# Layer 2's pair weights stand three groups ahead of the pair's products

## The chip, the cores and the metric

The kernel runs on one core of a Trainium2 chip. The metric is the device time of one execution in microseconds (us). Engines are named as in the profile: PE is TensorE (PEld its weight loads), ACT is ScalarE, DVE is VectorE, POOL is GpSimd, SP is SyncE.

## What is computed

A graph network of two attention layers and a two-layer perceptron, on 6250 nodes and 100,000 edges that come sorted by their destination, with a self-loop at each node. All numbers are float32. Cut to what matters:

```python
def gat_conv(x, src, dst, W, a_src, a_dst, bias, heads):
    h = (x @ W).reshape(n, heads, -1)
    alpha_s = (h * a_src[None]).sum(-1)
    alpha_d = (h * a_dst[None]).sum(-1)
    e = leaky_relu(alpha_s[src] + alpha_d[dst], 0.2)
    e = exp(e - segment_max(e, dst)[dst])
    alpha = e / (segment_sum(e, dst)[dst] + 1e-16)
    return segment_sum(h[src] * alpha, dst) + bias

h = maximum(layernorm(x), 0)
h = relu(gat_conv(h, src, dst, W1, ..., heads=4))    # 768 -> 256, layer 1
h = relu(gat_conv(h, src, dst, W2, ..., heads=1))    # 256 -> 256, layer 2
h = relu(h @ Wm1 + bm1)                              # 256 -> 256
out = x + h @ Wm2 + bm2                              # 256 -> 768
```

## The kernel before

**Tiles.** The nodes are cut into 49 node tiles of 128. The edges are cut into 782 edge tiles of 128; four edge tiles make a group (TPG = 4, NG = 196 groups), two of them a pair, so a group has pairs 0 and 1. Four groups, 16 edge tiles, carry on average the edges of one node tile. A layer's loop runs over the groups; each turn has two half-groups, one for each pair.

**One pair in layer 2.** POOL gathers the source nodes' rows from a table in HBM, one indirect DMA of 128 rows for each edge tile (`gather`, L666). A row holds the 256 features, the score, a one and the score's multiple. ACT makes the edge weights w: for each of the two tiles one Relu (L733) and one Exp (L735). DVE puts each edge's weight in the column of its destination (L739, `hw`). PE multiplies `hw` with the gathered rows G and adds into `o_ps` in PSUM (L760); each of the two float32 products shows as two passes in the profile.

**Sums and node steps.** Two groups share one `o_ps`. `take_sum` adds it into a running sum (DVE L777) and copies quarters of it to the node tiles that they belong to (ACT L786). When a node tile's sum is whole, `Node2.steps` carries it through the rest in six steps:

- step 0: self-loop and reciprocal on DVE (L1082, L1094)
- step 1: `o` on ACT (L1097), then two transposes on PE (L942)
- step 2: `rT` on ACT (L948), then the products with Wm1 on PE (L1106)
- step 3: `mT` on ACT (L1111); then on PE the bias into `y_ps` (L1055) and the first half of the product with Wm2 (L1116)
- step 4: DVE adds x to that half (L1120, called add_x below); then PE does the second half (L1055, L1116)
- step 5: DVE adds x to the second half (L1120), and SP sends the tile out

**The order.** Each engine runs its instructions in the order in which the program writes them, so the program's text is the schedule. The loop writes for each group: the gather of the group 8 ahead (AHEAD), pair 0, the node steps that are due, a sum if one is due; then pair 1, the steps and the sum of that half-group. Which half-group a sum or a step is due at is written out: sum u at half-group 4u + 11 (UP_AT), the six steps of node tile t at 8t + 19 plus 1, 2, 5, 8, 11 and 14 (STEPS_AT), with another table for the last node tiles. So every eight half-groups, over one node tile, the same things recur. Counted from 8t + 19 as position 3, so that a position is the half-group's number modulo 8, they are:

| position | what is written after the pair of this half-group |
|---|---|
| 0 | step 2 (rT, L1106) |
| 1 | step 5 (second add_x, out) |
| 2 | nothing |
| 3 | step 3 (mT, L1055, L1116), a sum |
| 4 | step 0 |
| 5 | step 1 (o, transposes) |
| 6 | step 4 (first add_x, L1055, L1116) |
| 7 | a sum |

The last two groups are written by `last_pairs`.

**Buffers.** 20 pairs of gathered rows fit in SBUF, so a gather waits until the pair 20 pairs before it has been multiplied; since gathers run 8 groups ahead of the pair being written, up to 40 edge tiles are gathered or under way. `w` has 4 buffers, `hw` 14 pairs, `o_ps` three banks. The transposes' PSUM tile `tp` and `y_ps` share two banks (tag "n") in turn; so step 3's L1055 of a node tile needs the add_x of step 5 of the node tile before.

In layer 1 `pair` does other work on DVE (L746 to L748) and nothing on ACT.

Of the kernel before, what the change touches and what calls it, by code (L numbers as in the profile page):

```python
# [30 lines left out]
NG = NQ  # L31
# [24 lines left out]
SOON_FROM, SOON_HELD = min(SOON), 16  # L56
BARE = 8
SLOPES, SLOPES_AT = 56, 150


UP_AT = {4 * u + 11: u for u in range(NU - 16)}
# [10 lines left out]
def kernel(  # L72
# [247 lines left out]
    def rows_in(layer):  # L320

        return gp.tile([P, 2, max(TW.values())], F32, name="G")[:, :, :TW[layer]]
# [40 lines left out]
    def soon_back(i):  # L363
        G = rows_in(1)
        nc.sync.dma_start(G.rearrange("p t c -> p (t c)"), soon_d[i])
        return G
# [242 lines left out]
    def fetch_rows(r):  # L609

        if r < NET // 16:
            drow[r] = rowsp.tile([P, 16 * P], BF16, name="drow")
            nc.sync.dma_start(drow[r], bcast(dmod_d, 16 * P, r * 16 * P))
# [19 lines left out]
    def layer_edges(layer, H, node, pre, matched, pre_pool):  # L633
# [4 lines left out]
        with tc.tile_pool(name=f"eg{layer}", bufs=5) as eg, \  # L638
# [12 lines left out]
            def tiles(g):  # L651

                return range(max(TPG * g, FIRST) - TPG * g, min(TPG * g + TPG, LAST) - TPG * g)

            def gather(g):
                if not 0 <= g < NG:
                    return
                for t in tiles(g):
                    k = TPG * g + t
                    soon = layer == 1 and k // 2 in SOON_AT  # L660
                    if k // 2 not in G:
                        G[k // 2] = (soon_back(SOON_AT[k // 2]) if soon else
                                     first_G.get(layer, {}).get(k // 2) or rows_in(layer))
                    if soon or k < FIRST + len(THERE.get(layer, ())):
                        continue
                    nc.gpsimd.indirect_dma_start(  # L666
                        out=G[k // 2][:, k % 2], out_offset=None, in_=table[layer],
                        in_offset=bass.IndirectOffsetOnAxis(ap=src_i[:, k:k + 1], axis=0))
# [51 lines left out]
                    e_ps[t][:, T, 3 * H:4 * H],  # L720
                    e_ps[t][:, T, :3 * H].rearrange("p t (h k) -> p t h k", k=3), AX.X, ALU.add)

            def pair(g, p):

                if 2 * p not in tiles(g):
                    return
                Gp = G.pop(TPG // 2 * g + p)
                if layer == 2:
                    u = g // 2
                    rows = slope[u // 8][:, u % 8 * P:(u % 8 + 1) * P]  # L730
                    w = sm.tile([P, 2, P], F32, name="w")
                    for t in range(2):
                        nc.scalar.activation(w[:, t], rows, AF.Relu, bias=Gp[:, t, HID + 2:])  # L733
                    for t in range(2):
                        nc.scalar.activation(w[:, t], w[:, t], AF.Exp, bias=Gp[:, t, HID:HID + 1])  # L735
                    hw = hwp.tile([P, 2, P], F32, name="hw")
                    for t in range(2):
                        k = TPG * g + 2 * p + t
                        nc.vector.scalar_tensor_tensor(hw[:, t], iota_ps, dcol[:, k:k + 1], w[:, t],  # L739
                                                       ALU.is_equal, ALU.mult)  # L740
                else:
                    e1, e2 = Gp[:, :, RW[1]:RW[1] + 4], Gp[:, :, RW[1] + 4:]
                    at = TPG * (g % 4) + 2 * p
                    rho, v, w = (e_ps[g // 4][:, at:at + 2, k * H:(k + 1) * H] for k in range(3, 6))
                    nc.vector.tensor_mul(v, e2, rho)
                    nc.vector.tensor_max(w, v, e1)  # L746
                    hw = hwp.tile([P, 2, H, C + 1], F32, name="hw")
                    nc.vector.tensor_mul(  # L748
                        hw, Gp[:, :, :RW[1]].rearrange("p t (h c) -> p t h c", h=H),
                        w.unsqueeze(3).to_broadcast([P, 2, H, C + 1]))  # L750
                u = g // 2
                if u not in o_ps:
                    o_ps[u] = ps.tile([P, RW[layer]], F32, name="o_ps", tag="o", bufs=3)
                for t in range(2):
                    k = 2 * p + t
                    if layer == 2:
                        l, r = hw[:, t], Gp[:, t]
                    else:
                        l, r = hot[g][:, k], hw[:, t].rearrange("p h c -> p (h c)")
                    nc.tensor.matmul(o_ps[u], l, r[:, :RW[layer]], start=(g % 2 == 0 and k == 0),  # L760
                                     stop=(g % 2 == 1 and k == tiles(g)[-1]))
# [36 lines left out]
            def gather_up(u):  # L798

                if u == NU - 1:  # L800

                    late.append(node.steps(NT - 1, None, run[0], o_ps.pop(u)))
                    return
                acc = take_sum(u)
                if u == NU - 2:
                    carry_over(acc)
# [45 lines left out]
            def last_pairs():  # L852

                acc = take_sum(NU - 2)
                before, = late
                pair(NG - 2, 0)
                next(before)
                carry_over(acc)
                next(before)
                next(before)  # L860
                pair(NG - 2, 1)
                next(before)
                pair(NG - 1, 0)
                pair(NG - 1, 1)
                last = node.steps(NT - 1, None, run[0], o_ps.pop(NU - 1))
                for of in (last, before, last, before, last, before, before, last, last):
                    next(of, 0)
                late.clear()

            for g in range(NG):  # L870
                t, j = divmod(g, 4)
                if layer == 2 and g >= NG - 2:
                    if g == NG - 2:
                        last_pairs()
                    continue
                if g == NG - 2:
                    at_end.append(g)
                gather(g + AHEAD)
                pair(g, 0)
                if g == NG - 1:  # L880
                    pair(g, 1)
                if g == NG - 2:
                    gather_up(NU - 2)
                advance(g)
                if taken_up(2 * g) is not None:
                    gather_up(taken_up(2 * g))
                if g <= NG - 4:
                    make_hot(g + 1)
                if g in (NG - 4, NG - 3):
                    make_hot(g + 2)  # L890
                if j == 0:
                    if layer == 1:
                        fetch_rows(t + 4)
                    node.prefetch(t)
                    meet(t + 1)
                    if t % 4 == 1:
                        fetch_slopes(t // 4 + 1)
                elif j == (2 if t < NT - 1 else 1):
                    node.ahead(t)
                elif j % 2:  # L900
                    make_mask((g + 7) // 2)
                if layer == 1:
                    for i, at in enumerate(SOON_GROUP):
                        for k, hits_at in ((2 * i, at - 10), (2 * i + 1, at - 6)):
                            if g == hits_at + 3 + (k % 2 == 0):
                                soon_whole(G, k)
                            if g == hits_at:
                                soon_hits(pre_pool, k)
                            if g == hits_at + 1 + (k % 2 == 0):
                                soon_missing(k)  # L910
                        if g == at - 13:
                            soon_sources(pre_pool, i)
                if g == NG - 3:
                    idle_ps.append(ps.tile([P, 4 * P], F32, name="idle_ps", tag="e"))
                if g >= NG - 3:
                    stay_warm(3)
                if g < NG - 1:
                    pair(g, 1)
                advance(g, 1)
                if j == 3:  # L920
                    join(t + 1)
                if taken_up(2 * g + 1) is not None:
                    gather_up(taken_up(2 * g + 1))
                if NG - 3 <= g < NG - 1:
                    stay_warm(3)
                hot.pop(g, None)
                if layer == 1 and g == SLOPES_AT:
                    slopes(pre_pool, 0, SLOPES)
                if layer == 1 and g == NG - 6:
                    first_sources(2)  # L930
# [77 lines left out]
    with tc.tile_pool(name="wmp", bufs=1) as wp, tc.tile_pool(name="x3", bufs=4) as xp, \  # L1008
# [140 lines left out]
        for stage in range(2):  # L1149
            first_hits(pre, 2, stage)  # L1150
        layer_edges(2, 1, Node2(), pre2, matched, pre)

    edges_stack.close()
# [310 lines left out]
```

## Time and profile before

| | us |
|---|---|
| median of 3 runs | 2594.48 |
| lowest and highest of them | 2586.76, 2594.98 |
| profiled execution, its own time | 2557.3 |
| its span in the profile | 2555.5 |

| | PE | DVE | ACT | POOL |
|---|---|---|---|---|
| busy in the whole span, us | 1718.3 | 1239.2 | 865.5 | 1528.5 |
| share of the span | 67% | 48% | 34% | 60% |

The mean granted PE clock was 0.804 of full speed. The profiled execution was 1.4% shorter than the median of the other runs. Layer 1 takes up the time from about 400 us; layer 2's first product starts at 1422.5 us, its last gather at 2503.5 us. In the profile "idle before" is the time for which an engine stood before an instruction, with what released it; "issue" means that nothing in the profile shows the cause, "remote" that it was an event without an instruction beside it. Ends of matmuls are modelled.

### The profile page before, as it was taken

To read this page: it belongs to the slowest core of one execution; us is meant where nothing else is said; L and a number is where in the kernel's file an instruction comes from. 1 tells how busy PE (TensorE), PEld (TensorE's weight loads), DVE (VectorE), ACT (ScalarE), POOL (GpSimd) and SP (SyncE) were. 2 spreads that over 40 slices of the span, in tenths; PEclk is the share of its full clock that TensorE was granted. 3 is DMA by queue.
4 is the path that set the end of the run, shared out by engine and by line. 5 is a ranking of instruction groups with operands and counts; after the bars stand their busy time and mean duration, and the time that the engine had idled before them with its cause. 6 is when DMAs were issued, how large, how long until landed. Compare 5 with 4: busy or idle time off the path is not lost. (4 is left out here: it accounts for less than half of the span.)

```text
span 2555.5 us, 24791 instructions
## 1 busy us (share of the span) xinstructions
PE 1718.3 (67%) x6948; PEld 1232.2 (48%) x6949; DVE 1239.2 (48%) x3356; ACT 865.5 (34%) x2796; POOL 1528.5 (60%) x1666
## 2 busy tenths in 40 slices
PE   9952768668667767758775546566666666656577
PEld 7731646546445545546553334344344444434344
DVE  7742667567666666566674323233233333333233
ACT  6730011011111111111112535455555555556455
POOL 5357465566666666665555566666666666666661
PEclk9975788778778778778877778778878878787778
DMA  9985344344444444444434244444444444444442
GB/s 352 349 269 167 94 130 127 106 130 129 120 127 137 124 121 126 124 122 128 121 84 149 79 119 126 133 135 125 129 137 125 131 135 135 131 127 134 120 132 75
DMA packets 141093, 355.46 MB, mean 139 GB/s; under 512 B 33731, under 2 KB 51324, under 8 KB 140948
## 3 DMA queue, kind: packets, MB, share of 16 engines
q0 software_dynamic: 75072, 211.10, 30.5%
q1 hardware_dynamic: 64506, 141.20, 16.5%
q10 hardware_dynamic: 1370, 1.48, 0.2%
q8 instruction: 59, 0.97, 0.2%
q14 instruction: 86, 0.70, 0.1%
HBM read 314.67 MB, written 38.99 MB: 138 GB/s over the span
## 5 line engine op out<-in xcount | busy, mean ns | idle before, releaser
L666 POOL DMA_INDIRECT G<-table,src_i x1507 | 1436.4, 953 | 851.5 <-issue 382.8
L760 PE MATMUL o_ps<-hw,hot 128*128 128x260 f32 x1564 | 496.5, 452 | 246.0 <-issue 159.7
L760 PE MATMUL o_ps<-G,hw 128*128 128x258 f32 x1564 | 465.8, 439 | 184.0 <-DVE hw L739 109.2
L739 DVE SCALAR_TENSOR_TENSOR hw<-iota_ps,dcol,w 128x128 f32<-128x128 f32 x782 | 247.5, 349 | 549.7 <-ACT w L735 368.7
L760 PEld LDWEIGHTS o_ps<-hw,hot 128*128 128x128 f32 x1564 | 331.9, 221 | 372.7 <-issue 213.1
L786 ACT ACTIVATE sum<-acc 32x260 f32<-32x260 f32 (+1 forms) x384 | 159.9, 417 | 1007.0 <-DVE acc L777 642.5
L760 PEld LDWEIGHTS o_ps<-G,hw 128*128 128x128 f32 x1564 | 326.0, 220 | 309.1 <-DVE hw L739 138.0
L390 PE MATMUL missing<-kept,soon_hit 128*128 128x268 f32 x1028 | 266.1, 413 | 50.9 <-issue 50.6
L748 DVE TENSOR_TENSOR hw<-G,e_ps 128x520 f32<-128x520 f32 x391 | 271.9, 695 | 30.6 <-DVE e_ps L746 15.8
L733 ACT ACTIVATE w<-slope,G 128x128 f32<-128x128 f32 x782 | 267.1, 389 | 46.2 <-issue 32.8
L735 ACT ACTIVATE w<-w,G 128x128 f32<-128x128 f32 x782 | 267.7, 388 | 28.9 <-remote 15.8
L1116 PE MATMUL y_ps<-wm,mT 128*128 128x384 f32 x392 | 187.4, 610 | 109.1 <-ACT mT L1111 95.7
L390 PEld LDWEIGHTS missing<-kept,soon_hit 128*128 128x128 f32 x1028 | 207.4, 204 | 102.2 <-issue 63.4
L1116 PEld LDWEIGHTS y_ps<-wm,mT 128*128 128x128 f32 x392 | 79.7, 225 | 217.4 <-ACT mT L1111 101.1
L448 PE MATMUL h_ps<-w,r 128*128 128x264 f32 (+1 forms) x588 | 139.2, 390 | 19.8 <-ACT r L438 13.5
L1120 DVE TENSOR_TENSOR y<-y_ps,xt 128x384 f32<-128x384 f32 (+1 forms) x98 | 54.1, 552 | 190.6 <-remote 157.6
L693 DVE TENSOR_TENSOR hot<-iota_ps,dcol 128x512 f32<-128x512 f32 x196 | 133.6, 682 | 24.4 <-remote 24.4
L448 PEld LDWEIGHTS h_ps<-w,r 128*128 128x128 f32 x588 | 109.1, 192 | 42.7 <-ACT r L438 15.2
L1111 ACT ACTIVATE mT<-tp,bm1c 128x128 f32<-128x128 f32 x98 | 30.4, 361 | 252.0 <-remote 184.0
L397 DVE SCALAR_TENSOR_TENSOR G<-G,soon_ok,missing 128x268 f32<-128x268 f32 x46 | 22.6, 492 | 187.0 <-remote 103.1
L1106 PE MATMUL tp<-rT,wm 128*128 128x128 f32 x392 | 59.6, 301 | 63.9 <-ACT rT L948 46.9
L746 DVE TENSOR_TENSOR e_ps<-e_ps,G 128x8 f32<-128x8 f32 x391 | 68.1, 174 | 53.4 <-remote 25.4
(420 smaller groups left out, 1286.8 us busy)
## 6 DMA issues: line engine op xcount, KB each, us to landing
xt<-in_x SPq DMA_DIRECT2D x96, 384.0 KB
drow<-dmod_d SPq DMA_DIRECT2D x49, 512.0 KB
G<-table,src_i POOLq DMA_INDIRECT x1507
xTt<-in_xT SPq DMA_DIRECT2D x49, 384.0 KB
out<-y SPq DMA_DIRECT2D x48, 384.0 KB
table<-kept SPq DMA_DIRECT2D x49, 134.0 KB
table<-kept SPq DMA_DIRECT2D x49, 129.5 KB
soon_d<-G SPq DMA_DIRECT2D x23, 268.0 KB
```

Source lines behind the costliest of these rows:

```text
L390: nc.tensor.matmul(soon_p[k], hit[:, T - there], kept[T], start=(T == there), stop=(T == NT - 1))
L448: nc.tensor.matmul(h_ps[:, :n], r[:, k], w1[:, k, :n], start=(k == 0), stop=(k == KI - 1))
L666: nc.gpsimd.indirect_dma_start(out=G[k // 2][:, k % 2], out_offset=None, in_=table[layer], in_offset=bass.IndirectOffsetOnAxis(ap=src_i[:, ...
L693: nc.vector.tensor_tensor(hot[g][:, T[0]:T[0] + n], iota_ps.unsqueeze(1).to_broadcast([P, n, P]), dcol[:, k:k + n].unsqueeze(2).to_broadca ...
L733: nc.scalar.activation(w[:, t], rows, AF.Relu, bias=Gp[:, t, HID + 2:])
L735: nc.scalar.activation(w[:, t], w[:, t], AF.Exp, bias=Gp[:, t, HID:HID + 1])
L739: nc.vector.scalar_tensor_tensor(hw[:, t], iota_ps, dcol[:, k:k + 1], w[:, t], ALU.is_equal, ALU.mult)
L746: nc.vector.tensor_max(w, v, e1)
L748: nc.vector.tensor_mul(hw, Gp[:, :, :RW[1]].rearrange("p t (h c) -> p t h c", h=H), w.unsqueeze(3).to_broadcast([P, 2, H, C + 1]))
L760: nc.tensor.matmul(o_ps[u], l, r[:, :RW[layer]], start=(g % 2 == 0 and k == 0), stop=(g % 2 == 1 and k == tiles(g)[-1]))
L786: nc.scalar.activation(done[t][r], acc[r], AF.Copy)
L1116: nc.tensor.matmul(y_ps, mT[:, j], wm2[:, j, s * half:(s + 1) * half], start=False, stop=(j == KH - 1))
```

## The change

The weights of a pair move from `pair` to a new function `weigh`, which is called for the pair three groups ahead in layer 2 (WEIGH = {1: 0, 2: 3}); `pair` takes what `weigh` has stored. Ahead of layer 2's loop `weigh` is called for groups 0 to 2. In layer 1 `weigh` runs where it ran. The numbers of instructions, the buffers and the tables UP_AT and STEPS_AT are the same.

```diff
+WEIGH = {1: 0, 2: 3}
...
-            def pair(g, p):
-
-                if 2 * p not in tiles(g):
+            weighed = {}
+
+            def weigh(g, p):
+
+                if g >= NG or (g, p) in weighed or 2 * p not in tiles(g):
                     return
                 Gp = G.pop(TPG // 2 * g + p)
                 if layer == 2:
...
+                weighed[g, p] = Gp, hw
+
+            def pair(g, p):
+
+                if 2 * p not in tiles(g):
+                    return
+                weigh(g, p)
+                Gp, hw = weighed[g, p]
                 u = g // 2
...
+            for g in range(WEIGH[layer]):
+                for p in range(2):
+                    weigh(g, p)
+
             for g in range(NG):
...
                 gather(g + AHEAD)
+                weigh(g + WEIGH[layer], 0)
                 pair(g, 0)
...
                 if g < NG - 1:
+                    weigh(g + WEIGH[layer], 1)
                     pair(g, 1)
```

What lies between the first two "..." inside `weigh` are the lines of `pair` that made w and hw, unchanged (L727 to L750 of the kernel before).

## The prediction

> **What bounds the kernel now.** I read the windows first, because the change touches only layer 2, which runs from the first product at 1422.5 us to the end. The columns are stretch, length, busy us (and instructions) of PE, PEld, DVE, ACT and POOL, then the granted clock, the DMA share and GB/s.
>
> ```profile
> 1424.00:2504.00 1080.00, 674.14 (x2390) 454.49 (x2389) 341.83 (x1029) 588.74 (x1898) 705.85 (x742) 0.79 0.44 129
> 2504.00:2555.00 51.00, 39.68 (x153) 24.99 (x151) 18.59 (x52) 26.67 (x85) 0.52 (x1) 0.92 0.15 51
> ```
>
> The first row is the body, the second the tail after the last gather. Nobody is full in the body: POOL is busy 705.85 of 1080 us, PE 674. The next view is POOL's timeline beside the others over one node tile. Columns: start, length, instruction, idle before it and what ended that.
>
> ```profile
> 2131.76 1.05 PE L1106 MATMUL tp<-rT,wm 128*128 128x128 f32 x8
> ...
> 2132.65 1.04 PE L760 MATMUL o_ps<-G,hw 128*128 128x258 f32 x4
> ...
> 2139.15 0.95 POOL L666 DMA_INDIRECT G<-table,src_i  x1 [0.30 <-issue]
> 2140.70 0.56 DVE L1120 TENSOR_TENSOR y<-y_ps,xt 128x384 f32<-128x384 f32 x1 [8.33 <-issue]
> 2141.17 1.12 DVE L739 SCALAR_TENSOR_TENSOR hw<-iota_ps,dcol,w 128x128 f32<-128x128 f32 x4
> ...
> 2141.57 2.95 PE L760 MATMUL o_ps<-G,hw 128*128 128x258 f32 x6 [7.89 <-issue]
> ...
> 2143.07 0.63 ACT L1111 ACTIVATE mT<-tp,bm1c 128x128 f32<-128x128 f32 x2 [8.74 <-PE o_ps L760]
> 2143.60 0.94 POOL L666 DMA_INDIRECT G<-table,src_i  x1 [3.50 <-ACT mT L1111]
> ```
>
> PE ended the product of y at 2130.2 (L1116, 2128.62 + 1.56), yet DVE's add of it (L1120) began only at 2140.70; PE ended L1106 at 2132.8, yet ACT's mT began at 2143.07. So signals from PE were seen 10 us late, while POOL issued 16 gathers from 2120.21 to 2139.15 (1.2535 us apart: 0.95 of work, 0.30 "issue") and then stood 3.5 us until it saw products free its buffers. DVE was held at L1120 with the next weights (L739) behind it, and PE stood 7.9 us for those weights. The cycle before (2120.21) looks the same; it lasted 23.39 us, which is 16 x 1.2535 + 3.3: one node tile. In the body 742 gathers take 1079 us, against 742 x 1.2535 = 930 unbroken: about 150 us of pauses, some 48. In the tail, without gathers, PE is busy 39.7 of 51 us and is not seen late.
>
> The waits from 1500 us on (us in total, times, longest):
>
> ```profile
> DVE hw L739 <- ACT w L735: 354.0, 130, 16.9
> ACT mT L1111 <- remote: 184.0, 22, 15.3
> DVE y L1120 <- remote: 157.6, 21, 11.9
> PE o_ps L760 <- DVE hw L739: 100.3, 28, 11.0
> PE y_ps L1116 <- ACT mT L1111: 95.7, 16, 14.2
> PE tp L1106 <- ACT rT L948: 46.9, 6, 10.5
> PE y_ps L1055 <- DVE y L1120: 32.6, 5, 11.6
> ```
>
> The largest row (354) is idle time of an engine that isn't full. What counts is PE's four: 100 us for hw, which the change addresses, and 95.7 + 46.9 + 32.6 = 175 us for node steps, which it does not. Following every PE gap of the body to its cause, I get 367 us: 111 in 18 stops for hw with DVE held at L1120, 33 in short waits for hw, 109 in 19 stops for mT, 63 in 9 for rT, 51 in 10 at L1055.
>
> **What the Trainium skill says.** "Perfetto Trace Analysis", Tensor Engine Instruction: the end shown for a matmul is estimated, and its semaphore update comes after PSUM's acknowledgment and has to propagate. So no bar shows a late signal; the 10 us above agree, but the page gives no such size. "TensorE: Matmul & The Clock Gate", What's actually happening: after about 3.4 us idle the array runs at half clock until it was busy about as long. The trace agrees: after a stop of 7.9 us six passes take 2.95 us, against 1.04 for four before it. "Perfetto Trace Analysis", Optimization Strategy: the same gap repeating can mean that there is no buffer for the next tile; POOL's 3.5 us are that.
>
> **The change part by part.** Nothing is added or removed: per pair ACT still does four activations of 386 ns (0.29 us apart, so 1.17 us), DVE two L739 of 350 ns, PE the same products. The orders of PE, POOL and SP are the same; DMAs and gathers are issued where they were.
>
> 1. Before the loop six pairs' weights stand ahead. PE's first product still waits for pair 0 alone, which ACT does first, and the rows are there (gathers lead by 40 tiles). The other five, 5 x 1.17 = 5.9 us of ACT, delay no node step, since the first sum is taken at half-group 11. I take 0; bounds -2 and +6.
>
> 2. The weights of pair h + 6 stand where those of pair h stood. Ahead of each node step on ACT and DVE stands as much new work as before, so those steps cost 0 more. Queued behind a held L1120, mT or rT is now a weight needed six pairs later. New on DVE: the weight buffers (14) make h + 6 wait for the products of pair h - 8; the sums already wait for the same products, and PE has six pairs in hand: 12 tiles at 0.435 us from start to start at full clock (0.87 at half), 5.2 to 10.4 us. I take 0.
>
> 3. The 18 stops (111 us). Their signal is of y's second half, added at position 1 of 8 in a node tile's half-groups. PE then stopped ahead of position 2; now it runs pairs 2 and 3 and stops at position 3, where L1055 needs the same add_x (its PSUM buffer) and L1116 needs mT. What is late next is exactly that. So a stop does not vanish: PE gains four tiles, 4 x 0.435 = 1.7 us (3.4 at half clock). This shortens the body only if it saves pauses. A tile in a cycle costs 23.39/16 = 1.46 us and without pauses 1.2535, so each tile gained saves 0.21 us: all 18 x 4 = 72 tiles would give 15 us. Where the stop moves for good to position 3, the cycle is 16 tiles again and the gain is 0. I take half, **-7.5 us**.
>
> 4. The short waits for hw (33 us) lie in the stretch after a pause in which PE's signals are seen promptly (under 1.5 us late for some 5 us). Less waiting there puts more of the chain into the prompt stretch and may spare a later stop. Bounds 0 and -33; I take a third, **-11**.
>
> 5. The tail: of 4.4 us in which PE stands there, 3.8 are for hw (2.42, 0.74 and 0.35 are the largest). All go: **-3.8**.
>
> Sum: -7.5 - 11 - 3.8 = **-22 us**. Against the profiled execution (2557.3 us, span 2555.5) that is 2535. The median shown is 2594.5, 1.5% above it; I put the same saving on the median: **2572 us**.
>
> **The rivals.**
> *The pauses fall much more.* hw is 144 of the 367 us that PE stands. If POOL's pauses fall in that share, 150 x 0.39 = 59 us; if POOL never pauses, 150 us, and the body is 930. For it: neither engine is full, so they hold each other, and a PE that is looser by six pairs loosens both. Against it: the stops for mT, rT and L1055 (223 us) depend on PE's own order, which stays. Time -45 to -150: 2445 to 2550.
>
> *The change does not do what it says: the lock of 16.* Each cycle ends at a stop that comes once per node tile, whichever it is, and POOL gets 16 tiles of credit per pause. Cycles that end for hw and for mT have the same 23.39 us, which speaks for it. Then only the tail remains, -4, with some noise: 2587 to 2602.
>
> *Slower: a second stop per node tile.* With hw out of the way PE enters the node steps with its signals elsewhere in POOL's cycle. If a cycle then ends after six or ten tiles (at rT, position 0, then at L1055, position 6) rather than after 16, POOL pauses twice in that tile. Each extra pause costs 3.3 us, and a stop at half clock with it. From three more pauses than are saved (9.9 us) the kernel is slower; if it befalls one tile in six, 8 x 3.3 = +26; one in three, 16 x 3.3 = +53. For it: waits of 10 to 15 us whose place follows no engine's work but the gathers. Against: about 48 pauses for 49 tiles, so no double ones now. Time 2602 to 2650.
>
> **How the numbers follow.** About 0.3% (7.8 us) is what a measurement of this kernel can tell from no change. Likeliest, the sum: -8 to -45, chance 0.40. Pauses fall much more: 0.22. Lock of 16: 0.15. Second stop: 0.23. So faster 0.62, same 0.15, slower 0.23. The range leaves out savings over 110 us (0.05) and losses over 20 us (0.13): 2485 to 2615. The likeliest case alone would give 2550 to 2587.
>
> **What would show it right or wrong.** Right: waits of L760 for hw fall from 100 us to under 20, those of L1116 for mT and of L1055 for y grow by most of what goes; POOL's 742 gathers still break after about 16, in 44 to 47 pauses of 3.5 us; tail under 48 us. The lock: 48 pauses and the body still 1079 us. Much faster: stretches of 30 gathers and more without a pause, POOL busy over 70% of the body. Slower: pauses after six or ten gathers, over 50 in all. Wrong altogether: PE's signals prompt under unbroken gathers, or L760 still waiting for hw by tens of us.

## Result and profile after

The changed kernel takes 2582.44 us (median of 17 runs, 2568.05 to 2591.84) against 2592.56 us for the kernel before (17 runs): ratio 0.9962, 95% interval 0.9945 to 0.9978. That is 10 us less (6 to 14), clear of noise, where 22 us were forecast.

The same program runs in two ways. On some occasions, those of the prediction and of the result among them, the kernel before takes about 2590 us and PE's signals are seen late; on others it takes about 2100 us and they are not. All runs of one comparison belong to one occasion. I call the two **late** and **prompt**. Most experiments fell on a prompt one.

The waits of PE in the profile after, from 1500 to 2500 us (us in total, times, longest). L1072, L1128, L1133 and L1137 are the lines that were L1055, L1111, L1116 and L1120; L736, L738, L742, L771, L788 and L797 were L733, L735, L739, L760, L777 and L786:

```profile
PE y_ps L1133 <- ACT mT L1128: 145.5, 19, 15.2
PE y_ps L1072 <- DVE y L1137: 124.9, 22, 14.8
```

No row of L771 waiting for hw is left; 97 us of it stood in the same stretch before. In its place the waits for mT grew from 96 to 146 us and those at the bias line (L1072) from 33 to 125. The groups of the whole profile say the same (line, engine, instruction, count, busy us, mean ns, then idle before it); first a line of before, then two of after:

```profile
L760 PE MATMUL o_ps<-G,hw 128*128 128x258 f32 x1564 | 465.8, 439 | 184.0 <-DVE hw L739 109.2
```

```profile
L771 PE MATMUL o_ps<-G,hw 128*128 128x258 f32 x1564 | 421.1, 416 | 39.9 <-DVE acc L786 18.8
L1133 PE MATMUL y_ps<-wm,mT 128*128 128x384 f32 x392 | 201.2, 648 | 190.4 <-ACT mT L1128 146.1
```

Where PE stops has moved; how fast layer 2 advances has not. POOL's gathers between 1500 and 2500 us, before and after (line, instruction, count, busy us, mean ns, idle before it):

```profile
L666 POOL DMA_INDIRECT G<-table,src_i x686 | 652.6, 951 | 348.3 <-issue 176.0 <-ACT mT L1111 83.2 <-ACT w L735 37.3
```

```profile
L667 POOL DMA_INDIRECT G<-table,src_i x683 | 646.8, 947 | 353.1 <-issue 212.1 <-ACT mT L1128 61.0 <-ACT w L736 27.8
```

686 and 683 gathers in the same 1000 us: the body gained nothing.

The traces' lists of instructions say more about POOL's pauses. Call it a pause when a gather starts over 1 us later than the usual 1.2535 us after the one before. Layer 2's last 742 gathers hold 51 pauses before and 55 after. Only 18 and 16 of these come after exactly 16 gathers; 9 and 16 come after ten or fewer. Every pause stands before the first gather of a pair, where POOL needs the buffer of the pair 20 pairs earlier. In 50 of the 51 and in all 55, the product that frees this buffer had ended before POOL's last gather even began; POOL went on 12.9 and 13.9 us after that end (medians). So POOL does not stand for PE to reach a product; by these times it stands until it sees that PE made it long ago.

The stretch after the last gather did gain; before and after, cut in the same way:

```profile
2504.40:2555.50 51.10, 39.28 (x151) 24.64 (x149) 18.18 (x52) 26.27 (x84) 0.12 (x1) 0.91 0.15 49
```

```profile
2521.70:2566.30 44.60, 33.37 (x144) 22.28 (x144) 14.61 (x39) 19.05 (x60) 0.10 (x1) 0.97 0.17 56
```

It is 44.6 us long, against 51.1 us: 6.5 us less. The profiled execution as a whole was longer (2568.05 us against 2557.3), since layer 2's first product, up to which the change alters nothing on PE, came 13 us later; from layer 2's first product to the end of the span it took 1130.9 us against 1133.0. So the whole times come from the medians, and the place of a gain from the profiles.

### The profile page after: what moved, and what is told of

Read it like the earlier page. It is cut to its first block, busy times and chain, and to the rows that moved or that the text cites. A ratio compares the mean times of both kernels' runs of the same rounds, so it can differ in the third digit from the quotient of the medians.

```text
span 2566.3 us, 24142 instructions
## 1 busy us (share of the span) xinstructions
PE 1697.2 (66%) x6947; PEld 1236.7 (48%) x6949; DVE 1241.0 (48%) x3356; ACT 866.3 (34%) x2796; POOL 1522.2 (59%) x1666
## 4 chain that ended last, share of the span: by engine, by line
another core or an unknown queue 22%; PE 22%; DVE 20%; ACT 16%; issue 15%; DMA 3%; POOL 2%; SPq 0%; POOLq 0%; DVEq 0%; ACTq 0%
PE o_ps L771 8%; ACT w L736 6%; ACT w L738 6%; PE h_ps L449 4%; DVE hot L694 3%; PE y_ps L1133 3%; DVE hw L751 3%; PE missing L391 3%; DVE soon_hit L381 2%; POOL G L667 2%; DMA G<-table,src_i 2%; DVE e_ps L749 2%; ACT sum L797 2%; DVE acc L788 2%
## 5 line engine op out<-in xcount | busy, mean ns | idle before, releaser
L771 PE MATMUL o_ps<-hw,hot 128*128 128x260 f32 x1564 | 503.9, 458 | 237.5 <-issue 148.9
L797 ACT ACTIVATE sum<-acc 32x260 f32<-32x260 f32 (+1 forms) x384 | 159.9, 417 | 1079.0 <-DVE acc L788 769.1
L742 DVE SCALAR_TENSOR_TENSOR hw<-iota_ps,dcol,w 128x128 f32<-128x128 f32 x782 | 248.8, 349 | 563.9 <-ACT w L738 366.7
L771 PEld LDWEIGHTS o_ps<-hw,hot 128*128 128x128 f32 x1564 | 333.6, 223 | 373.0 <-issue 198.8
L771 PE MATMUL o_ps<-G,hw 128*128 128x258 f32 x1564 | 421.1, 416 | 39.9 <-DVE acc L786 18.8
L771 PEld LDWEIGHTS o_ps<-G,hw 128*128 128x128 f32 x1564 | 326.4, 214 | 124.2 <-issue 37.5
L1133 PE MATMUL y_ps<-wm,mT 128*128 128x384 f32 x392 | 201.2, 648 | 190.4 <-ACT mT L1128 146.1
L738 ACT ACTIVATE w<-w,G 128x128 f32<-128x128 f32 x782 | 269.0, 388 | 49.4 <-ACT w L738 16.6
L736 ACT ACTIVATE w<-slope,G 128x128 f32<-128x128 f32 x782 | 266.8, 388 | 47.4 <-issue 32.8
L1133 PEld LDWEIGHTS y_ps<-wm,mT 128*128 128x128 f32 x392 | 84.2, 238 | 400.1 <-ACT mT L1128 178.4
L1137 DVE TENSOR_TENSOR y<-y_ps,xt 128x384 f32<-128x384 f32 (+1 forms) x98 | 54.1, 552 | 187.0 <-remote 151.2
L1072 PE MATMUL y_ps<-bm2r,ones_r 3*128 3x384 bf16 x98 | 34.4, 354 | 148.0 <-DVE y L1137 126.4
L1128 ACT ACTIVATE mT<-tp,bm1c 128x128 f32<-128x128 f32 x98 | 30.3, 360 | 239.7 <-remote 209.4
L788 DVE SCALAR_TENSOR_TENSOR acc<-acc,keep,o_ps 128x260 f32<-128x260 f32 (+1 forms) x192 | 91.3, 476 | 2.9 <-PE o_ps L771 1.7
```

The source lines that it names most:

```text
L788: nc.vector.scalar_tensor_tensor(acc, run[0], keep[:, u % 2:u % 2 + 1], o_ps.pop(u), ALU.mult, ALU.add)
L797: nc.scalar.activation(done[t][r], acc[r], AF.Copy)
L1133: nc.tensor.matmul(y_ps, mT[:, j], wm2[:, j, s * half:(s + 1) * half], start=False, stop=(j == KH - 1))
```

## Experiments

### The change itself on a prompt occasion

The two kernels as they are. They ran after the runs of the next section, to which the first expectation refers.

> The change itself. On a chip where the kernel before takes about 2590 us: 0.3 to 0.5% faster, POOL pausing after about 16 gathers. On a chip where the kernel before takes about 2103 us and POOL's gathers run unbroken at 1.2535 us: gathers are the bound, PE runs close behind them, and a weight three groups ahead waits for rows that have not landed, with the node steps queued behind it; so 0.4 to 0.6% slower, all of it after the last gather (28 us from the last gather's start to the end, against 17). Rival: the loss of the runs with tail_only and separate y banks came from something else in them, and the change is within 0.1% of before.

> The kernel before, for a profile on the same chip. Where it takes about 2103 us: gathers unbroken, DVE's add_x and ACT's mT within 2 us of the PE product that they need, 17 us from the last gather's start to the end. Where it takes about 2590 us: about 48 pauses of POOL, PE's signals up to 15 us late, as in the profile shown.

Measured: 2110.27 us against 2099.35, ratio 1.0052 (1.0039 to 1.0064). On a prompt occasion the change is **slower** by 11 us. Before and after have the same 599 gathers in the 750 us from 1300 us on, with no pause:

```profile
L666 POOL DMA_INDIRECT G<-table,src_i x599 | 568.5, 949 | 182.5 <-issue 66.7 <-ACT w L735 41.7 <-PE o_ps L760 30.8
```

```profile
L667 POOL DMA_INDIRECT G<-table,src_i x599 | 568.4, 949 | 182.5 <-issue 67.9 <-ACT w L738 43.9 <-PE o_ps L771 28.6
```

568.5 + 182.5 over 599 is 1.254 us each: POOL is the bound, and only what comes after its last gather can differ. From 2070 us, about the last gather's start in both, PE has 55 passes left before the change (first line) and 100 after it (second):

```profile
2070.00:2105.00 35.00, 15.42 (x55) 9.41 (x53) 6.55 (x17) 7.52 (x23) 2.83 (x3) 0.85 0.16 49
```

```profile
2070.00:2105.00 35.00, 26.15 (x100) 16.65 (x99) 8.23 (x20) 8.65 (x26) 0.95 (x1) 0.89 0.17 53
```

The timeline of the changed kernel shows why (start, length, instruction, idle before it and its releaser):

```profile
2067.23 0.40 ACT L736 ACTIVATE w<-slope,G 128x128 f32<-128x128 f32 x1 [1.09 <-DMA G<-table,src_i]
2067.96 0.65 DVE L742 SCALAR_TENSOR_TENSOR hw<-iota_ps,dcol,w 128x128 f32<-128x128 f32 x2 [2.98 <-ACT w L738]
2068.52 0.55 DVE L1137 TENSOR_TENSOR y<-y_ps,xt 128x384 f32<-128x384 f32 x1
2069.12 0.47 PE L1072 MATMUL y_ps<-bm2r,ones_r 3*128 3x384 bf16 x1 [2.58 <-DVE y L1137]
```

A weight on ACT waits for a row that has just landed; DVE waits 2.98 us for that weight; only then comes add_x, for which PE has been standing 2.58 us. The node steps are queued behind weights of a pair whose rows aren't there yet. Counted at each gather's start from 1300 to 2050 us, POOL was 4 to 10 tiles ahead of PE's finished products before the change (median 5) and 12 to 20 after it (median 16). So the lead of three groups, 12 tiles, holds PE 11 tiles back, and that is paid once, at the end: from the last gather's start to the end of the span it took 22.8 us before and 35.6 after. Both are longer than expected (17 and 28); the difference is about as expected.

### Ahead in the tail alone, and in the body alone

```diff
+            def lead(g):
+                return max(0, min(3, g - 180)) if layer == 2 else 0
...
-                weigh(g + WEIGH[layer], 0)
+                for q in range(g, g + lead(g) + 1):
+                    weigh(q, 0)
```

This is the tail alone, cut to pair 0. For the body alone `lead` returns `(3 if g < 180 else 0)` in layer 2.

> Weights stand ahead (1, 2, then 3 groups) only from group 181 on; up to there the order is that of the kernel before. Lock theory (each cycle of POOL is one node tile whatever stops PE; the gain of the change sits after the last gather): the stops for hw of about 110 us stay in the body, the stretch after the last gather is 44 to 48 us as after the change (51 before), and the time is 4 to 10 us under before, equal to the change within 4 us. Rival (the gain comes from saved pauses in the body): within 4 us of before.

> Weights stand three groups ahead up to group 179 and are made just before their products after that. Lock theory: hw waits gone in the body, 742 gathers still in about 1080 us, the stretch after the last gather 50 to 52 us: within 4 us of before. Rival (saved pauses): 6 to 12 us under before, like the change.

Both fell on a prompt occasion, for which the expectations give no number. Tail alone: 2114.03 us against 2102.93, ratio 1.0052 (1.0038 to 1.0065), just like the whole change. Body alone: 2103.15, ratio 0.9999 (0.9991 to 1.0007). So the loss lies wholly in the weights that lead at the end. What either does on a late occasion was **not measured**. After 2070 us tail alone leaves PE 101 passes, body alone 52:

```profile
2070.00:2109.00 39.00, 26.53 (x101) 16.88 (x100) 10.23 (x26) 11.46 (x35) 2.84 (x3) 0.87 0.17 55
```

```profile
2070.00:2109.00 39.00, 15.08 (x52) 9.35 (x52) 6.07 (x16) 7.47 (x23) 2.11 (x3) 0.83 0.13 37
```

### Twice the lead, on a late occasion

```diff
-WEIGH = {1: 0, 2: 3}
+WEIGH = {1: 0, 2: 6}
```

> WEIGH = 6 groups ahead instead of 3. Where before takes about 2100 us (gathers unbroken): if the loss is the node steps standing behind weights that wait for rows, it grows with the lead, one group being four gathers of 1.25 us; 12 us for 3 groups makes 4 us per group, so the stretch from the last gather's start to the end is about 40 us (28 with 3, 17 with 0) and the time 20 to 24 us over before. Rival (a fixed cost of standing ahead): 10 us over before, as with 3. Where before takes about 2590 us, lock theory: no difference in the body to 3 groups; 0 to 15 us under before.

Measured: 2582.46 us against 2584.51, ratio 0.9977 (0.9949 to 1.0004). Its gathers from 1500 to 2500 us, then PE's first wait:

```profile
L667 POOL DMA_INDIRECT G<-table,src_i x682 | 645.8, 947 | 354.6 <-issue 167.0 <-ACT mT L1128 128.3 <-ACT w L736 21.3
```

```profile
PE y_ps L1072 <- DVE y L1137: 313.1, 40, 8.9
```

682 gathers. The stops have moved again: PE stands 313 us at L1072 in 40 stops, for an add_x that is queued behind DVE's weight L742. L742 itself waits 440 us in 48 waits for an event that the profile does not name. From the order of the buffers I take it to be PE's late signal that one of the 14 hw buffers is free. A third place to stop, the same pace. From the last gather's start to the end 45.7 us pass here, 45.4 after the change and 51.9 before it, so the gain at the end is there too, though in the medians the 2 us are not clear of noise.

### Other banks for y, and the node steps spread

`y_ps` takes the two PSUM banks with tag "e", which layer 2 leaves idle, so that L1072 no longer waits for the add_x of the tile before:

```diff
-                if g == NG - 3:
+                if layer == 1 and g == NG - 3:
                     idle_ps.append(ps.tile([P, 4 * P], F32, name="idle_ps", tag="e"))
...
-                y_ps = ps.tile([P, half], F32, name="y_ps", tag="n")
+                y_ps = ps.tile([P, half], F32, name="y_ps", tag="e")
...
-                start_y(1, y_ps)
+                y_ps = start_y(1)
```

> The change, with both halves of y in PSUM banks of their own (the two that layer 2 leaves idle), so that L1055 (L1072 in the kernel after) no longer waits for add_x of the tile before. Lock theory: the stops at that line (137 us in 27 stops) go, those for mT at the same position take them over, cycles stay 16 gathers + 3.3 us: within 6 us of the change. Rival (that line is what bounds the cycle): 20 to 60 us faster than the change.

On a prompt occasion: 2113.04 us against 2102.93, ratio 1.0048 (1.0034 to 1.0062), as the change; it tells nothing of the cycle. Then, with those banks, the steps further apart:

```diff
-STEPS_AT = {t: [8 * t + 19 + k for k in (1, 2, 5, 8, 11, 14)] for t in range(NT - 2)}
+STEPS_AT = {t: [8 * t + 19 + k for k in (1, 2, 8, 15, 17, 19)] for t in range(NT - 2)}
```

> As the run with separate banks, and the node steps spread: STEPS_AT offsets 1, 2, 8, 15, 17, 19 instead of 1, 2, 5, 8, 11, 14, so that PE's transposes and L1106 have 6 and 7 half-groups instead of 3 before PE needs what ACT makes of them. Lock theory: no stop within one node tile is left, so POOL's pauses are no longer tied to 16 tiles; PE's stops fall from about 390 us to under 200, the body from 1080 to 950-1030 us, the whole 50 to 130 us under the change. Rival (the pauses are POOL's or the DMA's own, or late signals hit whatever waits for PE, so that the next wait takes over): within 15 us of the change.

It was run twice more:

> The kernel of the run with separate y banks and the node steps spread to offsets 1, 2, 8, 15, 17, 19, again. Where before takes about 2590 us, by the lock theory: POOL's pauses no longer tied to 16 tiles, PE's stops under 200 us, the whole 50 to 130 us under the change; rival: late signals hit the next wait, within 15 us of the change. Where before takes about 2103 us: 0.6% slower, as measured there.

> Separate y banks and the node steps spread to offsets 1, 2, 8, 15, 17, 19, with the weights three groups ahead. Where before takes about 2590 us, lock theory: within one node tile no place is left at which PE stops for ACT or DVE, so POOL's pauses are no longer tied to 16 gathers; the body per gather falls from 1.46 us to 1.28-1.40, the whole 50 to 130 us under before. Rival (late signals hit the next wait that exists, such as the weight buffers or the sums): 1.44 to 1.47 us per gather, within 15 us of before. Where before takes about 2100 us: 0.6 to 0.8% slower, as measured there.

All three comparisons fell on prompt occasions: 1.0061, 1.0076 and 1.0062 times before, 0.1 to 0.25% above the change alone. Offsets 1, 2, 9, 17, 18, 20 leave more room:

> Separate y banks and the node steps spread further: STEPS_AT offsets 1, 2, 9, 17, 18, 20, so 7 half-groups between the transposes and L1106 and 8 between L1106 and mT's product, more than the 16 tiles of a cycle together with the node products. Where before takes about 2590 us, lock theory: PE's stops under 150 us, gathers at 1.26 to 1.38 us each with pauses rarer than one per node tile, the whole 60 to 150 us under before. Rival (late signals hit the next wait): 1.44 to 1.47 us per gather, within 15 us of before. Where before takes about 2100 us, gathers being the bound: 0.6 to 1% slower, by the later node steps at the end.

> Separate y banks and STEPS_AT offsets 1, 2, 9, 17, 18, 20, for a chip where before takes about 2590 us. Lock theory: PE's stops under 150 us, gathers at 1.26 to 1.38 us each with pauses rarer than one per node tile, the whole 60 to 150 us under before. Rival (late signals hit the next wait): 1.44 to 1.47 us per gather, within 15 us of before. Where before takes about 2100 us: 0.5% slower, as measured there.

Prompt both times (1.0048 and 1.0044), and then a late one:

> As the run before of this kernel. Where before takes about 2590 us, lock theory: PE's stops under 150 us, gathers at 1.26 to 1.38 us each with pauses rarer than one per node tile, the whole 60 to 150 us under before. Rival (late signals hit the next wait): 1.44 to 1.47 us per gather, within 15 us of before. Where before takes about 2100 us: 0.5% slower, as measured there.

Measured there: 2570.70 us against 2575.54, ratio 0.9979 (0.9957 to 1.0001). The gain of 60 to 150 us did not come; the time is within 15 us of before, as the rival says. Gathers from 1500 to 2500 us, and PE's first wait:

```profile
L667 POOL DMA_INDIRECT G<-table,src_i x684 | 647.8, 947 | 353.0 <-issue 279.5 <-ACT w L738 40.9 <-PE o_ps L771 9.4
```

```profile
PE o_ps L771 <- DVE acc L788: 291.9, 41, 8.2
```

684 gathers. The waits at L1072 are down to 5 us and those at L1133 to 47 (5 put down to mT, 42 to a weight on ACT), and PE now stands 292 us in 41 stops for an o_ps bank. One cycle shows how:

```profile
2019.24 0.95 POOL L667 DMA_INDIRECT G<-table,src_i  x1 [0.30 <-issue]
2023.21 0.56 DVE L1137 TENSOR_TENSOR y<-y_ps,xt 128x384 f32<-128x384 f32 x1 [7.54 <-remote]
2023.68 0.47 DVE L788 SCALAR_TENSOR_TENSOR acc<-acc,keep,o_ps 128x258 f32<-128x258 f32 x1
2023.85 0.94 POOL L667 DMA_INDIRECT G<-table,src_i  x1 [3.66 <-issue]
2024.21 5.50 PE L771 MATMUL o_ps<-G,hw 128*128 128x258 f32 x16 [7.58 <-DVE acc L788]
```

DVE was held 7.5 us at add_x, now one or two half-groups after its product, with the sum that frees the bank queued behind it; everything was released about 4 us after the start of POOL's last gather. POOL started at 2000.49 and 2023.85 again: 23.36 us, 16 gathers and a pause. Of this kernel's 48 pauses 40 come after exactly 16 gathers, and of the 50 with the lead of six groups 34. In both, too, every pause stands before the first gather of a pair, and in all but one of the 98 the product that frees the buffer had ended before POOL's last gather began.

### No wait within a node tile

The step that was still close was moved too: offsets 1, 2, 9, 17, 18, 24 up to node tile 34, both halves of y made together in two banks, both add_x together in the last step.

The step that makes y, as it is there (cut):

```diff
+                if t < NT - 11:
+                    ys = [start_y(s) for s in range(2)]
+                    for s in range(2):
+                        for j in range(KH):
+                            product(ys[s], s, j)
+                    yield 1
+                    yield 1
+                    for s in range(2):
+                        add_x(ys[s], s)
...
```

> As the far spread, and add_x too stands 7 half-groups after its product: offsets 1, 2, 9, 17, 18, 24 up to node tile 34, both halves of y made together in two banks and both add_x together in the last step; x rows fetched one node tile later. No wait of PE, ACT or DVE on PE's work is left closer than 6 half-groups. Where before takes about 2590 us, lock theory: PE runs on, catches up with the gathers, POOL's pauses vanish for long stretches, 1.255 to 1.35 us per gather, the whole 60 to 150 us under before. Rival (the pauses are POOL's or the chip's own): 16 gathers and a pause of 3.5 us as ever, 1.44 to 1.47 us per gather, within 15 us of before. Where before takes about 2100 us: 0 to 1% slower.

> As the run before of this kernel (offsets 1, 2, 9, 17, 18, 24, halves of y together in two banks). Where before takes about 2590 us, lock theory: POOL's pauses vanish for long stretches, 1.255 to 1.35 us per gather, the whole 60 to 150 us under before. Rival (the pauses are POOL's or the chip's own): 16 gathers and a pause of 3.5 us as ever, 1.44 to 1.47 us per gather, within 15 us of before. Where before takes about 2100 us: 0.5% slower, as measured there.

> As the two runs before of this kernel. Where before takes about 2590 us, lock theory: POOL's pauses vanish for long stretches, 1.255 to 1.35 us per gather, the whole 60 to 150 us under before. Rival (the pauses are POOL's or the chip's own): 16 gathers and a pause of 3.5 us as ever, 1.44 to 1.47 us per gather, within 15 us of before. Where before takes about 2100 us: 0.4 to 0.5% slower, as measured there.

Three comparisons, all on prompt occasions: 1.0054, 1.0036 and 1.0044 times before. What it does on a late one was **not measured**. With the weights just in time from group 180 on:

> The kernel with no wait within a node tile (offsets 1, 2, 9, 17, 18, 24, halves of y together), and weights three groups ahead only up to group 179, just in time after that. Where before takes about 2590 us, lock theory: 1.255 to 1.35 us per gather, 60 to 150 us under before; rival: 1.44 to 1.47 us per gather, within 15 us of before. Where before takes about 2100 us: the loss of 0.4 to 0.5% of the kernels with weights ahead to the end lies after the last gather, so this one is within 0.1% of before, with 17 us from the last gather's start to the end instead of 28; rival (the moved node steps or the lead in the body cost something): 0.2 to 0.5% slower.

Prompt again: 2096.98 us against 2097.93, ratio 0.9994 (0.9986 to 1.0002). All of the loss is gone, as expected: no cost of the moved steps shows, and the loss lay in the lead at the end.

### Half the gathers

```diff
+                    if layer == 2 and t % 2 and g >= 4:
+                        continue
...
-                        l, r = hw[:, t], Gp[:, t]
+                        l, r = hw[:, t], Gp[:, t * (g < 4)]
```

> The change with half of layer 2's gathers left out from group 4 on: the second tile of each pair uses the rows of the first (the output is another one); PE, ACT and DVE do the same work. Lock theory, where before takes about 2590 us: a cycle is 8 gathers + 3.3 us = 13.4 us or PE's own 11 to 13.4 us for a node tile, so layer 2 takes 1130 - 48 x 10 = about 650 us, and the time is some 480 us shorter; PE's late signals are seen at each pause of POOL. Rival (signals are late for another reason than the stream of gathers): cycles stay near 23 us, the gain is under 100 us. Where before takes about 2103 us: PE becomes the bound, 11 to 12 us a node tile, layer 2 about 570 us against 900.

> The change with half of layer 2's gathers left out (a pair's second tile uses the rows of the first). Where before takes about 2590 us: lock theory, a cycle is 8 gathers + 3.3 us, 13.4 us for a node tile instead of 23.4, the whole about 480 us shorter, and layer 1 as slow as before. Rival (signals late whatever POOL does): cycles stay near 23 us and the gain is under 100 us. Where before takes about 2100 us: about 1814 us, as measured there.

Prompt, twice: 1813.99 and 1810.40 us (one execution each), some 287 us less than before, with PE busy 85% of the span. This agrees with the gathers being the bound of the prompt run. Whether late signals go with the stream of gathers, which it was made for, it couldn't tell.

## Why the prediction was wrong

**What bounds the kernel: right for the late occasions only.** There neither POOL nor PE is full; on prompt ones POOL never pauses (1.254 us per gather throughout) and is the bound alone. The prediction's own sign of being wrong altogether, PE's signals prompt under unbroken gathers, is what the prompt occasions show. Nothing in the one profile could say that.

**Steps 1 and 2 (0): no cost shows where the rows lead.** In the four late traces POOL was 24 to 39 tiles ahead of PE's finished products from 1500 to 2500 us (the prediction took the buffers' 40), more than the 12 tiles by which the weights lead. On prompt ones "as much new work as before" is true, but that work waits for its rows, and 11 us follow. The prediction had asked only whether the rows are there at the start of layer 2.

**Step 3 (-7.5): failed.** Its first half came true to the line: the stops for hw vanished and reappeared at L1072 and L1133, 142 us more in that stretch where 97 us had gone. The step that failed is the term that turned tiles gained into saved pauses. There were no fewer pauses (51 before, 55 after) and no more gathers in the same time (686 and 683). The product that POOL needed had been made some 13 us before POOL went on, so that PE makes it 1.7 us earlier can't by itself shorten the pause. Half of a bound was taken for it, beside the text's own remark that the gain is 0 where the stop moves for good.

**Step 4 (-11): failed in the same way.** The short waits went too, and the pace is the same. A third of a bound was taken for a wait on an engine that isn't the bound; the two steps were to give 18.5 us in the body and gave none.

**Step 5 (-3.8): right in kind, undersized.** 6.5 us in the two profiles. Of the 10 us in the medians (6 to 14) this is the only part that I can place; some 3 us more are within the interval and not placed. That the gain lies in the tail rests on profiles: the kernel with the lead in the tail alone, which would test it, never ran on a late occasion.

That 2582 us lies in the range of the likeliest case (2550 to 2587) is luck: the two steps that made up most of its sum gave nothing.

**The rivals' signs.** The result is nearest to the rival called the lock of 16, with the tail as its gain, but 10 us are more than its 4. Its picture holds only in part: in these two kernels most pauses do not come after 16 gathers. The reading "about 48 pauses ... so no double ones now" was a quotient of 150 and about 3.3 and not a count. There were 51, nine of them after ten gathers or fewer, so over 50 pauses could not be a sign of the slower rival. Nor does each pause cost 3.3 us: before the change they took 2.1 us after 12 gathers, 3.1 after 16 and 4.1 after 20 (means).

Four kernels, in which PE stopped for four different things, made 686, 683, 682 and 684 gathers in the same 1000 us. That PE's last stop doesn't set the pace is shown, and so is that POOL's pauses end with a late sight of products made before. **What sets the pace stays open.** That any wait once per node tile will do, my reading of the spread kernel, was only argued; the kernel that would decide it, with no such wait left, never fell on a late occasion. Why PE's signals are late on some occasions and not on others, no run tells.

## What to carry to other kernels

Where two engines hold each other in a cycle, ask of each stop that you remove whether the cycle gets shorter or only stops elsewhere: count the work per cycle before and after, and give a moved stop no gain. Count the pauses in the trace instead of dividing their sum by one of them, and look at each when the thing waited for was done: if it was done long before, making it earlier is not what ends the pause.

Preparing work ahead in the in-order queue of an engine is free only while its data lead too; where data arrive just in time, everything queued behind waits for them. The kernel with the lead up to group 179 lost nothing on prompt occasions. On late ones it was not run, and there it would give up the lead in the tail, where the profiles show the gain. And profile on more than one occasion: here the sign of the change differed.

## What was not expected of the hardware

The same program took 2592.56 us on one occasion and 2099.35 on another. The chip's number on record does not settle which: number 7 was late in one comparison (before: 2575.54 us) and prompt in another, half an hour later (2098.22 us).

A gather is as long on both (951 and 949 ns of POOL), the signals are not: add_x began 10.5 us after its product's end in the late profile that the prediction shows. In the profile of the change on a prompt occasion it began at once, 0.04 us after the product's end (2069.52 + 2.93 = 2072.45):

```profile
2069.52 2.93 PE L1133 MATMUL y_ps<-wm,mT 128*128 128x384 f32 x4
...
2072.49 0.56 DVE L1137 TENSOR_TENSOR y<-y_ps,xt 128x384 f32<-128x384 f32 x1 [0.59 <-PE y_ps L1133]
```

The traces also list when each semaphore (the counter by which one engine signals to another) was updated. For the kernel before on a prompt occasion, from 1300 to 2050 us, all 817 updates that PE's instructions make are listed, no two within 0.06 us. On the late one, from 1500 to 2500 us, 760 of 943 are listed, and 301 come within 0.06 us of the one before: they come in bunches. In the cycle that the prediction shows, none is listed between 2130.11 and 2142.82 us, and then eight in 0.35 us. This speaks for signals that were late themselves, and not only engines that were late to go on. The late list is not complete (the add_x at 2140.70 needed an update that it lacks), so what a late profile names as the end of a wait is less sure than in a prompt one.

The granted clock differs as well. It was 0.804, 0.878 and 0.934 where PE was busy for 67%, 80% and 85% of the span (before late, before prompt, half the gathers). It goes with PE's busy share in these three, so it need not be the cause.
